# Reordering operand preparation at layer ends, weight checks and attention norms in an attention and feed-forward kernel

## The chip, the cores and the metric

The kernel runs on one core of one Trainium2 chip. The metric is device time in microseconds (us). TensorE (PE) multiplies matrices, VectorE (DVE) and ScalarE (ACT) work element by element, GpSimd (POOL) does small and odd work, SyncE (SP) issues DMAs. Each engine executes its own instructions in the order in which the program gives them; engines wait for one another through semaphores.

## What is computed

A transformer block in float32 on `x` of shape 4 x 1024 x 256 (4 sequences, here called blocks 0 to 3): attention with 16 heads, then a gated feed-forward net with ternary weights, each between two layer norms and added to its input.

```python
x = x + layernorm(attention(layernorm(x), Wqkv, Wout))
h = silu(lin(n, w1, s1)) * lin(n, w2, s2)      # n = layernorm(x); 256 -> 1024, gated
h = gelu(lin(h, h1, sh1))                      # 1024 -> 1024, square layer one
h = gelu(lin(h, h2, sh2))                      # 1024 -> 1024, square layer two
x = x + layernorm(lin(h, w3, s3))              # 1024 -> 256
```

`lin` is a product with ternary weights (-1, 0, 1) times a scale for each output.

## The kernel before

**Attention** runs first over all four blocks, paced by exponentials on ScalarE and by TensorE. Side work is kept in chains of `Step`s, each with a `gap` (how many slots must pass since the chain's last step) that `side.take` gives out, one slot at a time, between pieces of the main loop. The function `ending(b, h, copy)` in the attention part makes the chain that projects half `h` of block `b`, normalises it and adds it to `x`: `gather` (statistics, VectorE), `root` (reciprocal root `rstd`, GpSimd, L108), `apply` (for block 3: `nb` on VectorE, L118, then scaling on ScalarE, L123) and `residual` (VectorE, L652). Block 3's chain is still running when the feed-forward part begins: there `side.take` is called once for each group of block 0's gated stage.

**Feed-forward** (`feed_forward`) goes through the blocks; each has four stages.

1. `gated`: 16 groups of 8 matmuls into one of three large PSUM tiles (`pg`, L936), then Silu on ScalarE (`sg`, L938) and the gated product on VectorE (`g`, L939). Lists named `steps` hold what is issued after each group.
2. `Layer.run`, twice: the square layers, by a Strassen-like scheme of seven products (k = 0 to 6) over quarter blocks, in 14 groups g of 16 matmuls (`ph`, L1015), k = g // 2 and r = g % 2 from group 6 on. Every operand is needed as a high and a low half: `high` rounds a raw tile on ScalarE (L906), `low` subtracts that from it on VectorE (L910). The last four groups end in `add`: group 10 and 11 sum PSUM into `w` (block (1, 1) of the output), group 12 and 13 into `u` (block (0, 1)), on VectorE (L1026), and `gelu` follows on ScalarE as two instructions (L1003). Groups 12 and 13 accumulate on in the same PSUM tiles that the sums of groups 10 and 11 read. What is issued after a group is in the lists `steps` and `extra`; `ending(layer, drop)` in the feed-forward part fills `extra` with the halves of output blocks that are ready (`split` gives `high` and `low` of one).
3. `finish`: products with `w3` (`pz`, L1119), first from blocks (0, 0), (1, 0), then (1, 1), (0, 1); then the layer norm and the sum with `x`.

**Checks** run beside this from block 1 on: a piece of a weight is loaded by SP (L1166), cast to int8 on ScalarE (`cast`, L1173) and compared on VectorE (`run`, L1179), 22 pieces in all; `checked(list, casts, runs)` says after which groups. If a weight is not a whole number, the result is computed again in another way; `judge` sums the verdicts in the last layer.

The queues of SP carry the weights of the square layers (`load_factor`, each issued when a product has released its ring), the checks' loads and the stores, in order. The `prepare` steps, spread over `extra`, norm and transpose the next block's input (`cq0hi`, `ck1lo` and the like, L882).

The order of everything is the order in which these functions are called. The group's end in `Layer.run` is:

```python
products(k, r, k == 5)
if k == 3:
    keep_copy("w", r)
elif k == 4:
    straight(1, r, at[r])
else:
    add(*(("w", 1, 1) if k == 5 else ("u", 0, 1)), r)
after(g)
```

Of the kernel before, what the change touches and what calls it, by code (L numbers as in the profile page):

```python
# [40 lines left out]
TPQ = NQ // P  # L41
# [89 lines left out]
def tile_fast(ctx: ExitStack, tc: tile.TileContext, x, wqk, wv, wo, w1, w1s, w2, w2s, h1, h1s, h2, h2s, w3, w3s, out, bad):  # L131
    nc = tc.nc
    B, S, D = x.shape
# [63 lines left out]
    with ExitStack() as actx, ExitStack() as rctx:  # L197
# [404 lines left out]
        def ending(b, h, copy):  # L602

            st = {}

            def transposes(c):
                def run():
                    if c == 0:
                        st["oT"] = work.tile([P, DC, NQ], F32, tag="oT", name=f"oT_{b}_{h}", bufs=1)
                        st["y"] = (both if h else work).tile([P, TPQ, D], F32, tag="y", name=f"y_{b}_{h}", bufs=1)  # L610
                    pt = misc(f"po_{b}_{h}_{c}")
                    for t in range(TPQ):
                        nc.tensor.transpose(pt[:, t * P : (t + 1) * P], on[h][:, t, c * P : (c + 1) * P], ident)
                    copy(st["oT"][:, c, :], pt)

                return run

            def project(t0):
                def run():
                    py = misc(f"py_{b}_{h}_{t0}").rearrange("p (t d) -> p t d", d=D)  # L620
                    for i in range(2):
                        for c in range(DC):
                            by_slots(py[:, i, :], st["oT"][:, c, (t0 + i) * P : (t0 + i + 1) * P], wo_sb[:, c, :], start=c == 0, stop=c == DC - 1)
                    (copy if b == B - 1 else to_scalar)(st["y"][:, t0 : t0 + 2, :], py)

                return run

            def gather(i):
                def run():
                    st["mv"] = norms.gather([st["y"][:, j, :] for j in range(i, i + 2)], i, st.get("mv"))  # L630

                return run

            def root():
                st["ln"] = norms.root(st["mv"])

            def apply(i0):
                def run():
                    if b == B - 1 and i0 == 0:
                        st["to"] = norms.shift(st["ln"])  # L640
                    for i in range(i0, i0 + 2):
                        if b == B - 1:
                            norms.scale(st["y"][:, i, :], st["y"][:, i, :], st["to"], i)
                        else:
                            norms.apply(st["y"][:, i, :], st["y"][:, i, :], st["ln"], i)

                return run

            def residual(i):
                def run():  # L650
                    xr = xs[b][:, h * TPQ + i : h * TPQ + i + 2, :]
                    nc.vector.tensor_add(xr, xr, st["y"][:, i : i + 2, :])  # L652

                return run

            steps = [Step(transposes(c), 1, work=1) for c in range(DC)] + [Step(project(t), 2, heavy=True) for t in range(0, TPQ, 2)]
            tail = (
                [Step(gather(i), 1, False, work=1.6) for i in range(0, TPQ, 2)] + [Step(root, 0, False, work=0.3)]
                + [Step(apply(i), 1, False, work=1.2) for i in range(0, TPQ, 2)] + [Step(residual(i), 1, False, work=1) for i in range(0, TPQ, 2)]
            )  # L660
            if b < B - 1:

                return steps + [Step(lambda: side.add(tail), 0, False)]
            return steps + ([Step(open_ffn, 0, False)] if h == NH - 1 else []) + tail

        class Side:

# [278 lines left out]
        class Layer:  # L946
# [33 lines left out]
            def low(self, k, i):  # L980
                return lambda: self.moving[k].low(i)

            def run(self, q, scale, extra):

                out, at = self.out, {}
                hi, lo = self.high, self.low
# [74 lines left out]
                for g in range(6, 14):  # L1061
                    k, r = g // 2, g % 2
                    if k == 5:
                        space(r)
                    products(k, r, k == 5)
                    if k == 3:
                        keep_copy("w", r)
                    elif k == 4:
# [4 lines that stand above are left out]
                return {n: out[n] for n in ((0, 0), (1, 0), (1, 1), (0, 1))}  # L1073

        class Tail:
# [11 lines left out]
            def apply(self, i0):  # L1087
                if i0 == 0:
                    self.to = norms.shift(self.ln)
                for t in range(i0, i0 + 2):  # L1090
                    norms.scale(self.z[:, t, :], self.z[:, t, :], self.to, t)
# [110 lines left out]
        def feed_forward():  # L1202

            chain = ends[B - 1, NH - 1]
            checks = Checks()
            tails = {}

            def split(o, i):
                return [lambda: o.high(i), lambda: o.low(i)]

            def ending(layer, drop):
                for at in ((0, 0), (1, 0), (1, 1), (0, 1)):
                    layer.out[at] = []
                ops = {at: Operand(layer.out[at], drop) for at in ((0, 0), (1, 0), (1, 1), (0, 1))}
                extra = {g: [] for g in range(14)}
                for g, at, i in ((7, (0, 0), 0), (10, (0, 0), 1), (11, (1, 0), 0), (12, (1, 0), 1)):
                    extra[g] += split(ops[at], i)
                return ops, extra

            def prepared(extra, steps):  # L1220
                for g, k in reversed(list(zip((3, 4, 4, 5, 6, 8, 9), range(7)))):
                    extra[g].insert(0, steps[k].run)

            def checked(steps, casts, runs):
                for g in casts:
                    steps[g].append(checks.cast)
                for g in runs:
                    steps[g].insert(0, checks.run)

            for b in range(B):  # L1230
                last = b == B - 1
                x = {}
                for at in ((0, 0), (1, 0), (0, 1), (1, 1)):
                    x[at] = []
                corner, low = Operand(x[0, 0]), Operand(x[1, 0])
                one = Layer(x, corner, low)
                steps = {g: [] for g in range(NH * HC)}
                if b == 0:
                    for g in steps:
                        steps[g].append(side.take)  # L1240
                    steps[7].append(lambda: until(lambda: "fb" in ffn))
                for g, runs in tails.items():
                    steps[g] += runs
                for g, runs in (
                    (7 if b == 0 else 6, split(corner, 0)), (8 if b == 0 else 7, split(corner, 1)), (9, split(low, 0)), (11, split(low, 1)),
                    (12, [one.t1(0)]), (14, [one.make2(0)]),
                ):
                    steps[g] += runs
                if b == 1:
                    steps[6] += [checks.load, checks.load]  # L1250
                if b:
                    checked(steps, (1, 6, 11), (3, 8, 13))
                gated(x, steps)
                until(lambda: made_factors[0] == len(corners) and "fb" in ffn)
                q = 2 * 7 * b
                ops, extra = ending(one, False)
                if b == 0:
                    for g in range(3, 12):
                        extra[g].append(side.take)
                if b:  # L1260
                    checked(extra, (3, 4, 10), (5, 6, 12))
                if not last:
                    prepared(extra, prepare(2 * b + 2, to_scalar))
                y = one.run(q, scales["h1"], extra)
                until(lambda: not chain[0])
                two = Layer(y, ops[0, 0], ops[1, 0])
                ops, extra = ending(two, True)
                if b:
                    checked(extra, (3, 4), (5, 6))
                if not last:  # L1270
                    prepared(extra, prepare(2 * b + 3, to_scalar))
                else:
                    for g, step in zip((8, 9), judge()):
                        extra[g].append(step.run)
                extra[12] += split(ops[1, 1], 0)
                extra[13] += split(ops[1, 1], 1) + split(ops[0, 1], 0)
                emit([two.t1(0), two.make2(0)])
                two.run(q + 7, scales["h2"], extra)
                tails = finish(b, ops, {0: split(ops[0, 1], 1)})
            assert checks.seen == len(checks.blocks)  # L1280
            side.flush()
# [325 lines left out]
```

## Time and profile before

| | |
|---|---|
| median of 3 runs | 1262.24 us (1261.6 to 1263.4) |
| profiled execution | 1258.22 us, span 1256.4 us |
| mean granted TensorE clock | 0.991 |
| feed-forward part | from about 611 us to the end |
| square layers' sums | L1026 on VectorE, 1.22 us each |
| Gelu pair | L1003 on ScalarE, 1.34 us |
| high half, low half | L906 1.04 us, L910 1.22 us |

A profile line gives start, duration, engine, line of the program, output and inputs with their shapes, and, in brackets, the idle time of the engine before it and what ended it. Chain lines give start, duration, engine, tile and line. Matmul ends are modelled, so successive matmuls seem to overlap.

### The profile page before, as it was taken

The page shows a single profiled execution, that of the slowest core. Times are in us where ns is not written, and L with a number is a line of the kernel's source. Part 1 is how long each engine was busy: PE and PEld are TensorE (multiplying, and loading weights), DVE is VectorE, ACT ScalarE, POOL GpSimd, SP SyncE. Part 2 cuts the span into 40 slices and gives each one's busy share as a digit, 9 for nine tenths or more (in the row PEclk, how much of TensorE's full clock was granted, in tenths as well). Part 3 has the DMA queues.
Part 4 walks back from the last instruction along what each step waited for, and adds up shares of the span by engine and source line. Part 5 has one row for each costly group of instructions (what it writes and reads, how often), then busy time and mean ns, then how long its engine had stood idle before and what let it go on. Part 6 is the DMA issues. An engine that isn't in the chain of part 4 may idle for free.

```text
span 1256.4 us, 20888 instructions
## 1 busy us (share of the span) xinstructions
PE 1194.4 (95%) x7848; PEld 720.9 (57%) x7848; DVE 822.5 (65%) x1448; ACT 887.6 (71%) x1051; POOL 205.8 (16%) x279
## 2 busy tenths in 40 slices
PE   7999999999999999988999999999999999999994
PEld 3333334333333333323568788787888878888783
DVE  3567567776578656766666656767568675784756
ACT  4888788888888888998556564575756756566651
POOL 6211125452444332000000000000000000000000
PEclk9999999999999999999999999999999999999997
DMA  5776645765665665454204341254513545135401
GB/s 145 178 181 161 159 116 138 174 170 147 158 160 144 167 171 130 94 119 142 101 1 138 130 146 61 97 167 152 180 59 108 172 129 190 51 101 184 137 15 37
DMA packets 78670, 163.63 MB, mean 130 GB/s; under 512 B 14688, under 2 KB 40928, under 8 KB 78560
## 3 DMA queue, kind: packets, MB, share of 16 engines
q1 hardware_dynamic: 68624, 131.27, 37.9%
q0 software_dynamic: 9408, 30.42, 7.7%
q8 instruction: 64, 1.05, 0.4%
q10 hardware_dynamic: 528, 0.52, 0.1%
q14 instruction: 46, 0.38, 0.1%
HBM read 98.71 MB, written 29.88 MB: 102 GB/s over the span
## 4 chain that ended last, share of the span: by engine, by line
PE 65%; DVE 12%; ACT 12%; issue 5%; SPq 2%; DMA 2%; POOL 1%; ACTq 0%; POOLq 0%; DVEq 0%
PE ph L1015 25%; PE acc L536 13%; PE s L528 8%; PE pg L936 8%; ACT e L529 6%; PE p L322 4%; DVE lo L910 3%; ACT hi L906 2%; PE py L322 2%; SPq L476 2%; PE pv L322 2%; ACT w L1003 2%; DVE w L1026 2%; DVE u L1026 1%; DVE top L545 1%
## 5 line engine op out<-in xcount | busy, mean ns | idle before, releaser
L529 ACT ACTIVATE e<-s 128x1024 f32<-128x1024 f32 x512 | 482.4, 1034 | 56.9 <-PE s L528 46.9
L536 PE MATMUL acc<-e,vaug 128*32 128x512 f32 x2048 | 256.7, 604 | 2.7 <-POOL vaug L506 2.7
L528 PE MATMUL s<-sq,sk 64*128 64x512 f32 x1024 | 184.3, 441 | 17.5 <-ACT e L529 14.6
L1015 PE MATMUL ph<-hi,sq 128*128 128x512 f32 x448 | 178.3, 398 | 2.6 <-DVE u L1026 2.3
L1015 PE MATMUL ph<-hi,sk 128*128 128x512 f32 x448 | 176.7, 394 | 0.0
L1015 PE MATMUL ph<-lo,sq 128*128 128x512 f32 x448 | 176.6, 394 | 0.0
L1015 PE MATMUL ph<-lo,sk 128*128 128x512 f32 x448 | 176.4, 394 | 0.0
L108 POOL TENSOR_TENSOR rstd<-ve,minus_half 128x4 f32<-128x4 f32 (+1 forms) x34 | 38.0, 1118 | 767.2 <-DVE ve L106 708.2
L528 PEld LDWEIGHTS s<-sq,sk 64*128 64x128 f32 x1024 | 85.3, 184 | 136.6 <-ACT e L529 113.9
L545 DVE TENSOR_TENSOR top<-top,e 128x512 f32<-128x512 f32 x192 | 135.0, 703 | 11.9 <-ACT e L529 6.5
L536 PEld LDWEIGHTS acc<-e,vaug 128*32 128x32 f32 x2048 | 49.4, 109 | 108.2 <-issue 100.2
L910 DVE TENSOR_TENSOR lo<-c,hi 128x1024 fp32r<-128x1024 f32 x48 | 58.4, 1224 | 79.5 <-ACT hi L906 79.5
L1015 PEld LDWEIGHTS ph<-hi,sq 128*128 128x128 f32 x448 | 84.2, 188 | 24.0 <-DVE u L1026 4.0
L910 DVE TENSOR_TENSOR lo<-g,hi 128x1024 fp32r<-128x1024 f32 x48 | 58.8, 1225 | 58.0 <-ACT hi L906 57.7
L1015 PEld LDWEIGHTS ph<-hi,sk 128*128 128x128 f32 x448 | 84.1, 188 | 20.0
L1015 PEld LDWEIGHTS ph<-lo,sk 128*128 128x128 f32 x448 | 84.1, 188 | 19.9
L1015 PEld LDWEIGHTS ph<-lo,sq 128*128 128x128 f32 x448 | 84.2, 188 | 19.1
L1003 ACT ACTIVATE c<-ph,h_scale 128x512 f32<-128x512 f32 x64 | 40.6, 685 | 47.3 <-PE ph L1015 47.3
L938 ACT ACTIVATE sg<-pg,w_scale 128x512 f32<-128x512 f32 x64 | 43.5, 687 | 36.3 <-PE pg L936 33.6
L939 DVE SCALAR_TENSOR_TENSOR g<-pg,w_scale,sg 128x512 f32<-128x512 f32 x64 | 47.8, 747 | 30.1 <-ACT sg L938 30.0
L322 PE MATMUL p<-xT,wqk_sb 128*32 128x512 f32 x512 | 60.8, 593 | 5.6 <-ACT wqk_sb L210 2.6
L1119 PE MATMUL pz<-w_sb,lo 128*128 128x256 f32 x256 | 62.8, 287 | 3.2 <-DVE lo L910 3.2
(189 smaller groups left out, 1785.0 us busy)
## 6 DMA issues: line engine op xcount, KB each, us to landing
sq<-h_f SPq DMA_DIRECT2D x56, 512.0 KB, 3.8
sk<-h_f SPq DMA_DIRECT2D x56, 512.0 KB, 4.4
w<-in_h_dram POOLq DMA_DIRECT2D x32, 256.0 KB, 5.7
h_f<-wr POOLq DMA_DIRECT2D x16, 512.0 KB, 4.4
x<-in_h_dram SPq DMA_DIRECT2D x16, 512.0 KB, 3.5
top_d<-top SPq DMA_DIRECT2D x30, 256.0 KB, 2.3
folded<-top_d SPq DMA_DIRECT2D x30, 256.0 KB, 3.5
h_f<-wr POOLq DMA_DIRECT2D x16, 384.0 KB, 3.7
```

What stands on the lines that cost most here:

```text
L322: nc.tensor.matmul(o[j : j + SLOT, :], w[:, j : j + SLOT], i, **flags)
L528: nc.tensor.matmul(s[:, a, :], stacks[1, g % 2, u][r, c * P : (c + 1) * P], stacks[0, g % 2, u][r, h * NQ : (h + 1) * NQ], start=True, sto ...
L529: nc.scalar.activation(pair(k)[:, u], s, AF.Exp)
L536: nc.tensor.matmul(acc[SLOT * i : SLOT * (i + 1), :], vaug[g % 2][:, c, i, :], pair(k)[:, i // 2, i % 2, :], start=c == 0, stop=c == NT - 1)
L545: nc.vector.tensor_max(top, top if c > 1 else pair(k - 2)[:, :, :, 0:P], pair(k)[:, :, :, 0:P])
L910: nc.vector.tensor_sub(self.lo[i].t, self.raw[i].t, self.hi[i].t.bitcast(F32))
L936: nc.tensor.matmul(p[:, k, :], homes[n][d][:, m * P : (m + 1) * P], half[:, d, :], start=d == j == 0, stop=d == DC - 1 and j == 1)
L938: nc.scalar.activation(sg, p[:, 0, :], AF.Silu, scale=scales["w1"][:, m : m + 1])
L939: nc.vector.scalar_tensor_tensor(x[i, h][c // 2].t[:, c % 2, :], p[:, 1, :], scales["w2"][:, m : m + 1], sg, ALU.mult, ALU.mult)
L1003: nc.scalar.activation(o.t[:, j, :], (o.t if src is None else src)[:, j, :], AF.Gelu, scale=scale[:, m : m + 1])
L1015: nc.tensor.matmul(p[:, j, :], w, half, start=start and c == n == 0, stop=c == HC // 2 - 1 and n == 1, skip_group_check=True,)
L1119: nc.tensor.matmul(p[:, j, :D], half[:, (t0 + j) * P : (t0 + j + 1) * P], homes["w3"][c], start=c == order[0] and n == 0, stop=c == order[ ...
```

## The change

In `Layer.run`, a new list `early` is issued after a group's matmuls and ahead of its sum, copy or Gelu. The halves that `ending` put into `extra` for groups 10, 11 and 12 go into `early`; in layer two also those of block (1, 1), in groups 12 and 13. In block 1's gated stage the casts after groups 1 and 6 and the runs at 3 and 8 are dropped; the checks follow in the later places, one place later each. The first `apply` of block 3's attention endings gets a gap of 2 slots in place of 1; two conditions (`opened.ready` and an `until` before group 5's extra work in block 0) keep the order of what depends on it.

In the streams of the engines, TensorE's and GpSimd's order is unchanged; ScalarE, VectorE and SP have the moves named here.

```diff
@@ -656,12 +656,14 @@
             steps = [Step(transposes(c), 1, work=1) for c in range(DC)] + [Step(project(t), 2, heavy=True) for t in range(0, TPQ, 2)]
             tail = (
                 [Step(gather(i), 1, False, work=1.6) for i in range(0, TPQ, 2)] + [Step(root, 0, False, work=0.3)]
-                + [Step(apply(i), 1, False, work=1.2) for i in range(0, TPQ, 2)] + [Step(residual(i), 1, False, work=1) for i in range(0, TPQ, 2)]
+                + [Step(apply(i), 2 if b == B - 1 and not i else 1, False, work=1.2) for i in range(0, TPQ, 2)] + [Step(residual(i), 1, False, work=1) for i in range(0, TPQ, 2)]
             )
             if b < B - 1:
 
                 return steps + [Step(lambda: side.add(tail), 0, False)]
-            return steps + ([Step(open_ffn, 0, False)] if h == NH - 1 else []) + tail
+            opened = Step(open_ffn, 0, False)
+            opened.ready = lambda: not ends[b, 0][0]
+            return steps + ([opened] if h == NH - 1 else []) + tail
 
         class Side:
 
@@ -980,7 +982,7 @@
             def low(self, k, i):
                 return lambda: self.moving[k].low(i)
 
-            def run(self, q, scale, extra):
+            def run(self, q, scale, extra, early):
 
                 out, at = self.out, {}
                 hi, lo = self.high, self.low
@@ -1063,6 +1065,7 @@
                     if k == 5:
                         space(r)
                     products(k, r, k == 5)
+                    emit(early.get(g, ()))
                     if k == 3:
                         keep_copy("w", r)
                     elif k == 4:
@@ -1213,9 +1216,9 @@
                     layer.out[at] = []
                 ops = {at: Operand(layer.out[at], drop) for at in ((0, 0), (1, 0), (1, 1), (0, 1))}
                 extra = {g: [] for g in range(14)}
-                for g, at, i in ((7, (0, 0), 0), (10, (0, 0), 1), (11, (1, 0), 0), (12, (1, 0), 1)):
-                    extra[g] += split(ops[at], i)
-                return ops, extra
+                extra[7] += split(ops[0, 0], 0)
+                early = {g: split(ops[at], i) for g, at, i in ((10, (0, 0), 1), (11, (1, 0), 0), (12, (1, 0), 1))}
+                return ops, extra, early
 
             def prepared(extra, steps):
                 for g, k in reversed(list(zip((3, 4, 4, 5, 6, 8, 9), range(7)))):
@@ -1248,12 +1251,14 @@
                     steps[g] += runs
                 if b == 1:
                     steps[6] += [checks.load, checks.load]
-                if b:
+                if b == 1:
+                    checked(steps, (11,), (13,))
+                elif b:
                     checked(steps, (1, 6, 11), (3, 8, 13))
                 gated(x, steps)
                 until(lambda: made_factors[0] == len(corners) and "fb" in ffn)
                 q = 2 * 7 * b
-                ops, extra = ending(one, False)
+                ops, extra, early = ending(one, False)
                 if b == 0:
                     for g in range(3, 12):
                         extra[g].append(side.take)
@@ -1261,10 +1266,12 @@
                     checked(extra, (3, 4, 10), (5, 6, 12))
                 if not last:
                     prepared(extra, prepare(2 * b + 2, to_scalar))
-                y = one.run(q, scales["h1"], extra)
+                if b == 0:
+                    extra[5].insert(0, lambda: until(lambda: not chain[0]))
+                y = one.run(q, scales["h1"], extra, early)
                 until(lambda: not chain[0])
                 two = Layer(y, ops[0, 0], ops[1, 0])
-                ops, extra = ending(two, True)
+                ops, extra, early = ending(two, True)
                 if b:
                     checked(extra, (3, 4), (5, 6))
                 if not last:
@@ -1272,10 +1279,11 @@
                 else:
                     for g, step in zip((8, 9), judge()):
                         extra[g].append(step.run)
-                extra[12] += split(ops[1, 1], 0)
-                extra[13] += split(ops[1, 1], 1) + split(ops[0, 1], 0)
+                early[12] += split(ops[1, 1], 0)
+                early[13] = split(ops[1, 1], 1)
+                extra[13] += split(ops[0, 1], 0)
                 emit([two.t1(0), two.make2(0)])
-                two.run(q + 7, scales["h2"], extra)
+                two.run(q + 7, scales["h2"], extra, early)
                 tails = finish(b, ops, {0: split(ops[0, 1], 1)})
             assert checks.seen == len(checks.blocks)
             side.flush()
```

## The prediction

> **What bounds the kernel now.** I read the engine totals first, then who TensorE waited for from 500 us on, then the chain of waits that ended last, then single timelines.
>
> ```profile
> PE 1194.4 (95%) x7848; PEld 720.9 (57%) x7848; DVE 822.5 (65%) x1448; ACT 887.6 (71%) x1051; POOL 205.8 (16%) x279
> ```
>
> TensorE is the bound and the change takes no matmul away, so only its gaps can be won. All the edits lie in the feed-forward part (about 611 us to the end), where it waits little (total us, times, longest):
>
> ```profile
> PE pg L936 <- DVE g L939: 4.5, 4, 2.2
> PE pz L1119 <- DVE lo L910: 3.2, 8, 0.5
> PE ph L1015 <- DVE u L1026: 2.3, 4, 0.6
> PE py L322 <- DVE ck1lo L882: 1.0, 1, 1.0
> ```
>
> Matmul ends are modelled and overlap, so I price a gap from start to start, less the usual pitch (228 ns for 512 columns, about 114 for 256). From the chain, the gated stage of block 1 against that of block 2 (start, us, what):
>
> ```profile
> 777.58 12.71 PE pg L936 x56
> ...
> 791.48 3.91 DMA x<-in_w_dram
> ...
> 797.88 12.75 PE pg L936 x48
> ...
> 934.48 29.05 PE pg L936 x128
> ```
>
> Block 1 spends 33.06 us (777.58 to 810.64) where block 2 spends 29.05: a transfer for the weight check stands in the chain. The end of layer two, block 1:
>
> ```profile
> 906.68 1.23 DVE w L1026
> 907.93 1.34 ACT w L1003 x2
> 909.27 0.95 ACT hi L906
> 910.24 1.23 DVE lo L910
> 911.47 1.15 DVE w L1026
> ...
> 926.62 1.22 DVE lo L910
> ...
> 928.45 1.14 DVE lo L910
> 929.63 4.85 PE pz L1119 x39
> ```
>
> VectorE and ScalarE hand work to and fro: sum, Gelu, high half, low half, next sum. TensorE waits at the end for the last low half. At the end of layer one:
>
> ```profile
> 866.93 1.14 DVE u L1026
> 868.12 29.99 PE ph L1015 x128
> ```
>
> The next layer's second product needs the PSUM bank that the last sum reads. In block 3's attention tail, ScalarE's timeline (start, us; in brackets its idle time):
>
> ```profile
> 640.87 0.69 ACT L938 ACTIVATE sg<-pg,w_scale 128x512 f32<-128x512 f32 x1 [0.18 <-PE pg L936]
> 645.45 1.09 ACT L123 ACTIVATE y<-y,nb,rstd 128x256 f32<-128x256 f32 x2 [3.88 <-DVE nb L118]
> 646.45 0.67 ACT L938 ACTIVATE sg<-pg,w_scale 128x512 f32<-128x512 f32 x1
> ```
>
> ScalarE stood 3.88 us before the norm's scaling, with a Silu (L938) queued behind it that TensorE needed.
>
> [...] Here the granted clock is 0.50 from 797.88 to 801.30 (pitch 427 ns), after a start-to-start gap of only 2.56 us; a gap of 1.43 us (627.52) had no such price. [...] The second `rstd` took 2.04 us beside a low half, the first 1.01[...].
>
> **Part 1: the dropped checks.** Block 1's cast (L1173) after group 6 and its run (L1179) before the work of group 8 go; the other check slots of the gated stages stay, all checks move up by one, and one more falls into block 3's second layer. The cast waited for its DMA, and Silu, product and TensorE waited behind it. Price: the gap's 2.33, then slow pitches 0.36 + 6 x 0.20 + 0.13, **4.0 us**, as 33.06 - 29.05. The two loads stay after group 6 and landed at 796.66 at the latest; the next cast ran at 804.95, so it waits for nothing. The late check (1.05 ScalarE, 1.22 VectorE, its load one place later on SP) sits where blocks 1 and 2 run one without a TensorE gap: 0. Bounds 3.5 to 4.1.
>
> **Part 2: the norms one step later.** No instruction is added. For half 0, `ck1hi` and `ck1lo` no longer stand behind `nb`, which waited for GpSimd (625.89); they can start after `g` at 625.62 instead of 625.97, so `py` starts **0.35** earlier. For half 1, VectorE runs two products, then `nb`; ScalarE runs the next Silu at 642.7 instead of 646.45. Unshifted: products at 644.27 and 644.93; `nb` 645.6; scaling 645.8 to 646.9; high half to 647.85; low half to 649.1; the third product ends at 649.77. The gap at 645.06 stays, that at 647.95 goes, group 15 starts at 649.8 instead of 651.00, and lasts 1.94. The layer starts at 651.74 instead of 653.40: **1.66**. What is late next is that third product, behind the moved scaling. Sum 2.0, bounds 0.5 to 3.
>
> **Part 3: halves ahead of sums.** In groups 10, 11, 12 (13 in layer two) `high` and `low` come before the sum and its Gelu, on both engines; nothing is added. Steps from the trace, start to start: sum to Gelu 1.26, Gelu pair to high 1.25, high to low 1.06, low to the next on VectorE 1.14.
>
> The cost first: the sum of group 10 now follows a low half. In block 1, layer two, `ck1lo` starts at 905.68, so the low half at 906.28 and the sum at 907.42, 0.74 later than 906.68.
>
> Layer one's end: the last sum no longer has a Gelu, a high and a low half before it, and ends before the second product asks. The gap goes: 0.77, 0.73, 0.69, 0.78 by block, each with 0.11 for the first pitch. But in blocks 1 to 3 a cast stands on ScalarE between Gelu 10 and the high half of group 11 (0.95). So the sum of group 11 in block 1: 853.49 + 1.26 + 1.25 + 0.95 + 1.06 + 1.14 = 859.15, ending 860.37; group 13's matmuls, which accumulate into the bank it reads, are due at 860.01. A **new wait** of 0.40 + 0.11 in three blocks; behind it on TensorE is all the rest. Block 0 has no cast: margin 0.6. Net 0.88 + 0.33 + 0.29 + 0.38 = **1.9**.
>
> Layer two's end (no cast): 907.42 + 4.70 = 912.12 for sum 11, ending 0.7 before group 13 needs it; + 1.26 + 1.25 + 1.06 = 915.69, two low halves, sum 12 at 917.96; + 1.25 Gelu + 1.25 high + 1.06 low + 1.13: sum 13 at 922.65; + 1.25 + 1.25 + 1.06 low half at 926.21, `z` at 927.35, last low half 927.95 against 928.36: 0.41. The earlier small gap (920.92) goes, but TensorE only arrives sooner at the same last wait. Block 3 has no `ck1lo`: shift 0.55, gain 0.6. Sum 3 x 0.41 + 0.6 = **1.8**. Nothing to gain or to lose for DMA queues: factor loads follow TensorE.
>
> The steps of part 3 not seen in the trace (order reversed): bounds from -2 (the new wait twice as long, no gain at layer two) to 7.5 (no new wait, 1.2 from each layer two). I take the worked 3.7.
>
> **Sum:** 4.0 + 2.0 + 1.9 + 1.8 = 9.7 us. The profiled execution took 1258.22 (span 1256.4), the runs' median is 1262.24; taken off that, **1252.5**.
>
> **Rivals.** (a) Halves only trade places: the 0.74 and the new wait eat part 3. Then 6.0, 1256.2. For it: the two engines' work between first sum and last low half is the same. Against: fewer hand-overs. (b) The new wait doesn't come and layer two gains 1.15 each: 9.7 + 1.5 + 2.8 = 14.0, 1248.2. (c) The dropped check's wait comes back at the next cast: 9.7 - 4.0 = 5.7, 1256.5; the landing times speak against. (d) Slower: sum 11 comes late for group 13 in all eight layers, by so much that the clock halves after it. At the price of 797.88, 4.0 each, 32 us less the 6 of parts 1 and 2: 1288. It beats the gains from about 1.2 us more a layer than I worked out; against: sum 11 ends within 0.4 of its time, and the halves' blocks have long been ready. (e) The steps move but the waits stay: no change, 1262.
>
> **How the numbers follow.** Mine 0.64, (a) 0.13, (b) 0.08, (c) 0.05, (d) 0.05, (e) 0.05. 0.2% is 2.5 us, about what a measurement of this kernel can tell from no change. Mine, (a), (b), (c) are faster, less 0.02 for a bad draw: 0.88 faster, 0.06 same, 0.06 slower. My own case is 1250 to 1255; to hold 8 in 10 with (a) and a part of (b), 1248.5 to 1257.5.
>
> **What would show it.** Right: block 1's gated stage takes 29 us with the clock at 1.00; no wait of `ph` on the last `u`; a wait of `ph` on `w` of 0.3 to 0.5 in three first layers; last low half of layer two some 22.5 us after its first sum is due (23.0 now); the scaling behind two Silus. Wrong: waits of `ph` on `w` above 1 us or in layer two, a cast waiting for its transfer, or a half clock before 1230 us.

## The result, and the profile after

The change makes the kernel faster. The median fell from 1261.92 us (6 runs, 1257.83 to 1263.4) to 1252.88 us (6 runs, 1248.23 to 1254.59), a ratio of 0.9926 with a 95% interval of 0.9904 to 0.9949. The profiled execution took 1248.23 us with a span of 1246.4 us and a mean granted clock of 0.993, 10.0 us less than the one before.

The engine totals are the same work in a shorter span:

```profile
PE 1190.4 (96%) x7848; PEld 719.9 (58%) x7848; DVE 821.7 (66%) x1448; ACT 888.0 (71%) x1051; POOL 206.0 (17%) x279
```

TensorE's waits from 500 us on (total us, times, longest) show what changed. Line numbers are 2 to 3 higher than before: `pg` 938, `hi` 908, `lo` 912, Gelu 1005, `ph` 1017, sums 1028, `pz` 1122.

```profile
PE pz L1122 <- DVE lo L912: 2.8, 7, 0.5
PE pg L938 <- DVE g L941: 1.4, 2, 0.8
PE ph L1017 <- DVE w L1028: 0.8, 3, 0.4
PE py L322 <- DVE ck1lo L884: 0.7, 1, 0.7
```

`pg` behind `g` fell from 4.5 to 1.4 us, the four waits of `ph` for the last `u` are gone (2.3), and a wait that did not exist, `ph` for `w`, stands in three places: the predicted new one.

The chain of waits of block 1's gated stage is now one piece of TensorE work, with no transfer in it, where there were pieces of 12.71 and 12.75 us with a DMA between them:

```profile
773.60 29.02 PE pg L938 x128
```

The end of layer one in block 1, from the same chain (start, us, what; the dots stand for pieces called "issue", short ones of 0.02 to 0.04 us here, and in the next view for longer stretches too):

```profile
845.47 1.22 DVE w L1028
...
846.72 1.34 ACT w L1005 x2
848.05 0.94 ACT whole L1176
848.99 0.96 ACT hi L908
...
849.97 1.23 DVE lo L912
851.20 1.14 DVE w L1028
...
852.39 37.38 PE ph L1017 x160
```

After the Gelu of group 10 comes the check's cast (`whole`), then the high half, the low half and only then the sum of group 11, for which TensorE waits until 852.39. From there TensorE runs 37.4 us in one piece, over the border to the next layer and its second group, where it used to stop (0.96 us from start to start at 868.12 before). The end of layer two, block 1:

```profile
899.15 1.15 DVE w L1028
...
906.36 0.94 ACT hi L908
...
908.47 1.22 DVE lo L912
909.69 1.15 DVE u L1028
...
919.01 0.68 DVE z L1127
919.70 1.14 DVE lo L912
...
920.88 4.83 PE pz L1122 x39
```

The last low half is still what TensorE waits for, only sooner. And ScalarE's timeline in block 3's attention tail (start, us; idle time in brackets):

```profile
639.94 0.69 ACT L940 ACTIVATE sg<-pg,w_scale 128x512 f32<-128x512 f32 x1 [0.19 <-PE pg L938]
641.75 0.69 ACT L940 ACTIVATE sg<-pg,w_scale 128x512 f32<-128x512 f32 x1 [1.12 <-DVE st L98]
644.84 1.09 ACT L123 ACTIVATE y<-y,nb,rstd 128x256 f32<-128x256 f32 x2 [2.40 <-DVE nb L118]
645.84 1.03 ACT L908 CAST hi<-g 128x1024 fp32r<-128x1024 f32 x1
646.78 0.68 ACT L940 ACTIVATE sg<-pg,w_scale 128x512 f32<-128x512 f32 x1
```

In the traces before and after, VectorE's 1426 and ScalarE's 1042 tile-writing instructions start in the order in which the program gives them, by the tiles they write, so a Silu waits with the scaling that is given ahead of it. Two Silus now precede the scaling. It waits 2.40 us rather than 3.88; the Silu that TensorE needs soonest is no longer behind it, but the third one is.

**Stage by stage.** I cut each trace at the start of the first matmul of a stage. "Layer one" runs to the start of layer two's second group of 16 matmuls (the prediction's "second product", in truth the second half of the first one), so that it holds the wait for the last sum; "end of layer two" runs from the first `pz` to the next block's first `pg` (block 3: to the end of VectorE's last instruction). The changes against before, us:

| stage | before | after | e1 | e2 | e3 | e8 |
|---|---|---|---|---|---|---|
| gated, block 0 | 42.53 | -2.03 | -0.02 | -2.04 | -0.02 | +0.01 |
| gated, block 1 | 33.06 | -4.04 | -4.04 | +0.05 | -1.37 | -4.05 |
| layer one, blocks 0, 1, 2, 3 | 57.74, 57.65, 57.68, 56.48 | -0.87, -0.22, -0.16, -0.15 | 0 to -0.03 | 0 to -0.06 | -0.76, -0.21, -0.16, -0.15 | 0 to +0.01 |
| rest of layer two, blocks 0 to 3 | 49.40, 49.45, 49.49, 48.74 | -0.12, -0.11, -0.10, -0.09 | within 0.01 | within 0.01 | -0.11, -0.12, -0.10, -0.08 | 0 to -0.02 |
| end of layer two, blocks 0, 1, 2, 3 | 16.87, 16.75, 16.73, 29.47 | -0.38, -0.43, -0.44, -0.61 | within 0.02 | within 0.02 | -0.38, -0.40, -0.42, -0.60 | +0.03 to -0.06 |

The column "after" adds up to -9.75 us. The gated stages of blocks 2 and 3 are unchanged (29.06 and 29.03). The spans differ by 10.04: a further 0.57 us arose before the feed-forward part, in code that is the same, and 0.28 went the other way after VectorE's last instruction (5.43 us to the end before, 5.71 after). The attention part reproduces badly: the first `pg` came at 610.87 us before, at 610.30 after, and anywhere between 612.39 and 617.69 in the ten experiments, whose attention code is the same. So single times scatter by some microseconds, while the stages after it repeat to about 0.06 us, but for a half-clock stretch in block 1's gated stage that some executions lack (e3, below). I take the size of an effect from the stages, and the sign for the whole kernel from the timed ratio; e6 shows where one profile's stages mislead.

### The profile page after: what moved, and what is told of

It reads as the page before. It is cut to its first block, busy times and chain, and to the rows that moved or that the text cites. A ratio compares the mean times of both kernels' runs of the same rounds, so it can differ in the third digit from the quotient of the medians.

```text
span 1246.4 us, 20894 instructions
## 1 busy us (share of the span) xinstructions
PE 1190.4 (96%) x7848; PEld 719.9 (58%) x7848; DVE 821.7 (66%) x1448; ACT 888.0 (71%) x1051; POOL 206.0 (17%) x279
## 4 chain that ended last, share of the span: by engine, by line
PE 67%; ACT 11%; DVE 10%; issue 5%; SPq 3%; DMA 2%; POOL 1%; ACTq 0%; POOLq 0%; DVEq 0%
PE ph L1017 27%; PE acc L536 12%; PE pg L938 8%; PE s L528 8%; ACT e L529 6%; PE p L322 4%; SPq L476 3%; DVE lo L912 2%; PE py L322 2%; ACT hi L908 2%; PE pv L322 2%; DVE top L545 1%; PE pz L1122 1%; DVE w L1028 1%; PE po L575 1%
## 5 line engine op out<-in xcount | busy, mean ns | idle before, releaser
L1017 PEld LDWEIGHTS ph<-hi,sq 128*128 128x128 f32 x448 | 84.1, 188 | 21.6 <-DVE w L1028 2.1
```

The source lines that it names most:

```text
L1017: nc.tensor.matmul(p[:, j, :], w, half, start=start and c == n == 0, stop=c == HC // 2 - 1 and n == 1, skip_group_check=True,)
```

## The experiments

My theory: three independent gains, the transfer's wait (4.0), the norms' order (2.0) and the halves' order (3.7, with a new wait that the cast makes). The rivals to be told apart were those of the prediction, and for single parts those that the expectations name.

**e1: only the checks dropped.** In the kernel before, the first of the two casts finds no weight loaded and does nothing, so one check leaves block 1's gated stage; it follows later, and all 22 are made in both kernels.

```diff
-                if b:
+                if b == 1:
+                    checked(steps, (11,), (13,))
+                elif b:
                     checked(steps, (1, 6, 11), (3, 8, 13))
```

> The kernel before with only the two early checks of block 1 dropped. My account: the gated stage of block 1 goes from 33.06 to about 29.05 us with the clock at 1.00, nothing else moves, about 4.0 us in all (ratio 0.9968). Rival (c), the wait comes back at the next cast: the stage stays above 32 us.

Measured: median 1259.66 us, ratio 0.9977 [0.9964, 0.999]. Block 1's gated stage takes 29.02 us, and no other stage moves by more than 0.03. The wait does not come back at the next cast: rival (c) is out.

**e2: only the norms one step later.**

```diff
-                + [Step(apply(i), 1, False, work=1.2) for i in range(0, TPQ, 2)]
+                + [Step(apply(i), 2 if b == B - 1 and not i else 1, False, work=1.2) for i in range(0, TPQ, 2)]
...
+            opened.ready = lambda: not ends[b, 0][0]
...
+                if b == 0:
+                    extra[5].insert(0, lambda: until(lambda: not chain[0]))
```

> The kernel before with only the norms of block 3 one step later (and the two conditions that keep their order). My account: the gated stage of block 0 goes from 42.53 to about 40.5 us, all other stages as before, 2.0 us in all. Rival, the GpSimd wait is only moved to another waiter: the stage keeps 42 us or more.

Measured: 1258.86 us, ratio 0.998 [0.9968, 0.9991]. Block 0's gated stage takes 40.49 us, 2.04 less, and nothing else moves by more than 0.06.

**e3: only the halves ahead of the sums.**

```diff
+                    emit(early.get(g, ()))
...
-                for g, at, i in ((7, (0, 0), 0), (10, (0, 0), 1), (11, (1, 0), 0), (12, (1, 0), 1)):
-                    extra[g] += split(ops[at], i)
+                extra[7] += split(ops[0, 0], 0)
+                early = {g: split(ops[at], i) for g, at, i in ((10, (0, 0), 1), (11, (1, 0), 0), (12, (1, 0), 1))}
...
-                extra[12] += split(ops[1, 1], 0)
-                extra[13] += split(ops[1, 1], 1) + split(ops[0, 1], 0)
+                early[12] += split(ops[1, 1], 0)
+                early[13] = split(ops[1, 1], 1)
+                extra[13] += split(ops[0, 1], 0)
```

> The kernel before with only the halves ahead of the sums. My account: 3.7 us in all. From the first matmul of layer one to the second product of layer two: 0.9 less in block 0, 0.2 to 0.3 less in blocks 1 to 3, with a wait of TensorE for the sum w of group 11 of 0.4 to 0.5 there and none in block 0 (a transfer in block 1's gated stage keeps its 4 us). Layer two's end: 0.4 less per block, 0.6 in block 3. Rival (a), work only trades places: below 1 us in all.

Measured: 1258.97 us, ratio 0.9976 [0.9961, 0.999]. TensorE's waits (lines here are 2 lower than after) have the new wait and the earlier last low half:

```profile
PE pz L1120 <- DVE lo L910: 2.9, 7, 0.5
...
PE ph L1015 <- DVE w L1026: 0.8, 3, 0.4
```

Layer one and layer two gain 1.69 and 1.80 us (with the rest of layer two, which belongs to layer one's wait, as said below). Rival (a), places only traded, is out, and so is (b), since the new wait is there. What I did not expect stands in block 1's gated stage. The check's transfer is still waited for, yet the stage lost 1.37 us. TensorE's timeline:

```profile
799.77 0.50 PE L936 MATMUL pg<-ck1hi,ck0hi 128*128 128x512 f32 x1 [2.10 <-DVE g L939]
...
800.34 0.40 PE L936 MATMUL pg<-ck1hi,ck0lo 128*128 128x512 f32 x1
```

The matmuls after the wait take 0.40 us, where those of before took 0.63 in the same place:

```profile
798.47 0.63 PE L936 MATMUL pg<-ck1lo,ck0hi 128*128 128x512 f32 x1
```

The gap is 2.49 us from start to start here and was 2.56 before; the granted clock after it stays at 1.00 and was 0.50. So 2.7 of the 4.0 us are the wait itself, and 1.4 are a slow clock that it brings only in some executions (e2 has it, with a stage of 33.11 us).

**e8: all checks kept, one load earlier.** This tells the transfer from the work of the check.

```diff
-                    steps[6] += [checks.load, checks.load]
+                    steps[2].append(checks.load)
+                    steps[6].append(checks.load)
```

> The kernel before with all its checks, the first check's load issued after group 2 of block 1's gated stage instead of after group 6. If the stall was the wait for the transfer: the stage falls from 33.06 to 29.1 us and the clock stays 1.00, 4.0 us in all, with no check dropped. If the cast's and the check's own work (1.05 and 1.22 us) made it: it stays above 31 us.

Measured: 1258.04 us, ratio 0.9966 [0.9952, 0.9979]. With all checks in their places, the chain has the whole gated stage of block 1 in one piece:

```profile
781.45 29.02 PE pg L936 x128
```

So the dropped cast and comparison cost TensorE nothing by themselves; the loss was the transfer that came too late for the cast. Moving one load is worth as much as moving the check to a later place.

**e4: layer one's third cast after group 8.** From here on the edits are against the changed kernel.

```diff
-                    checked(extra, (3, 4, 10), (5, 6, 12))
+                    checked(extra, (3, 4, 8), (5, 6, 12))
```

> The changed kernel with the check's cast in the first square layer moved from group 10 to group 8. If the cast between the Gelu of group 10 and the high half of group 11 makes the new wait of TensorE for w: it is gone in blocks 1 to 3, layer one and its boundary are 0.5 to 0.6 us shorter in each, 1.5 us in all against the changed kernel. Rival, the 0.74 us delay of the sum of group 10 is enough alone: the wait stays, less than 0.5 us in all.

Measured: 1250.57 us, ratio to the kernel before 0.9912 [0.9886, 0.9938]. TensorE's waits have no `ph` for `w` any more:

```profile
PE pz L1122 <- DVE lo L912: 2.8, 7, 0.5
PE pg L938 <- DVE g L941: 1.4, 2, 0.8
PE py L322 <- DVE ck1lo L884: 0.7, 1, 0.7
```

Layer one is 0.50, 0.54 and 0.64 us shorter in blocks 1 to 3 than with the change, and within 0.04 us the same in block 0, which has no cast. Without the cast there is no new wait; whether the cast alone makes it, e5 tells.

**e5: the second half of block (0, 0) prepared after group 8** in place of ahead of group 10's sum.

```diff
-                early = {g: split(ops[at], i) for g, at, i in ((10, (0, 0), 1), (11, (1, 0), 0), (12, (1, 0), 1))}
+                extra[8] += split(ops[0, 0], 1)
+                early = {g: split(ops[at], i) for g, at, i in ((11, (1, 0), 0), (12, (1, 0), 1))}
```

> The changed kernel with the halves of block (0, 0)'s second tile issued after group 8 in place of ahead of the sum of group 10. My account: the sum of group 10 starts when its matmuls end (0.55 to 0.75 us sooner), the wait for w of group 11 in blocks 1 to 3 is gone (0.5 each), and the last low half of layer two comes about 0.7 us sooner in each block: 1.5 + 2.7 = about 4.2 us less than the changed kernel, gaps at the end of layer two close to nothing. Rival, ScalarE and VectorE are full through groups 8 to 10 and the sum stays late: below 1 us.

Measured: 1249.38 us, ratio to before 0.9891 [0.9865, 0.9916]. Against the change, layer one is 0.53, 0.79 and 0.59 shorter in blocks 1 to 3, though the cast stands where it stood: the new wait needs both the cast and the later sum of group 10. The end of layer two is 0.88, 0.73, 0.66 and 0.47 shorter, so the rival is out. But layer two of block 3 lost 1.11. Its waits and VectorE's timeline say why:

```profile
PE pz L1122 <- DVE lo L912: 1.1, 4, 0.3
PE pn L1196 <- DVE total L1192: 1.1, 1, 1.1
```

```profile
1199.60 1.22 DVE L912 TENSOR_TENSOR lo<-c,hi 128x1024 fp32r<-128x1024 f32 x1
1200.74 0.18 DVE L1192 TENSOR_REDUCE total<-misses 128x1 f32<-128x30 f32 x1
```

The verdict's sum (`total`) stood behind the moved low half, and a matmul of `judge` (`pn`), next on TensorE, stood for it. My expectation missed that: it looked at the sums and halves and not at the third thing queued on VectorE there. The net gain, summed over the stages, is 3.3 us.

**e7: e5 and e4 together.**

```diff
+                extra[8] += split(ops[0, 0], 1)
...
-                    checked(extra, (3, 4, 10), (5, 6, 12))
+                    checked(extra, (3, 4, 8), (5, 6, 12))
```

> The changed kernel with both moves, the cast after group 8 and the second tile's halves after group 8. If the two moves remove the same wait in layer one: as with the second move alone, within 0.3 us of stage time, or a little worse where group 8 becomes crowded. If they add up: a further 1.5 us less.

Measured: 1250.41 us, ratio to before 0.9905 [0.9868, 0.9942]. Every stage is within 0.06 us of e5's. The two edits remove the same wait. What e5 gives beyond e4 is layer two's end, and 0.25 us more in block 2's layer one.

**e6: the new wait made longer.** The cast after group 10 of layer one is issued three times in blocks 1 to 3; the two repeats write the same values again.

```diff
+                    for _ in range(2):
+                        extra[10].append(lambda: nc.scalar.copy(checks.st["i", checks.made - 1], checks.st[checks.made - 1]))
```

> The changed kernel with the cast after group 10 of layer one repeated twice more (the same cast of the same data) in blocks 1 to 3. My account: each repeat delays the sum of group 11 by 0.95, so TensorE's wait for it grows from 0.4 to about 2.3 us in each of the three layers, 5.7 us in all if the clock stays; if a start-to-start gap of about 2.5 us is enough to halve the clock, as at 797.88 in the kernel before, 1.7 us more in each, up to 10.8 us in all. Rival, the wait for w is not set by this cast: below 2 us.

Measured: 1264.08 us, ratio to before 1.002 [1.0006, 1.0033]: slower than the kernel before. The waits of `ph` for `w` grew from 0.8 us in all to

```profile
PE ph L1017 <- DVE w L1028: 7.3, 3, 2.5
```

Layer one is 3.74, 2.16 and 2.15 us longer than with the change. The windows of 3.41 us right after the three gaps (busy time of TensorE, its weight loads, VectorE, ScalarE and GpSimd; granted clock; DMA share; GB/s):

```profile
858.45:861.86 3.41, 3.41 (x9) 2.75 (x10) 1.13 (x1) 2.25 (x3) 0.00 (x0) 0.59 0.00 0
1014.36:1017.77 3.41, 3.41 (x15) 2.78 (x16) 1.12 (x1) 2.26 (x3) 0.00 (x0) 1.00 0.00 0
1167.62:1171.03 3.41, 3.41 (x15) 2.80 (x16) 1.13 (x1) 2.25 (x3) 0.00 (x0) 1.00 0.02 5
```

The first gap, 2.78 us from start to start, is followed by a slow clock and nine matmuls; the other two, of 2.82 and 2.91, are longer and are followed by the full clock and fifteen. In this execution two of the three gaps cost only the wait, and by its stages it is still 1.7 us faster than the kernel before. It is not typical: its granted clock of 0.991 is the highest of the 20 timed runs, whose mean is 0.987 (0.990 in the 29 runs of the kernel before beside them). The difference of 0.003, over 1260 us, is 3.8 us of lost clock; a stretch of 3.41 us at half clock loses 1.7, so I estimate about two more such stretches per run than in the kernel before. The timed ratios put the loss against the change at 0.0094, about 12 us (7 to 16 with the two intervals), which is about 4 us for each gap (2.4 to 5.4). Rival (d) thus describes a real mechanism, a cast chain that turns the reordering into a loss, and its price of 4.0 us fits the timed runs.

**e9: e5, and `judge`'s first step one group earlier**, to take away e5's loss.

```diff
-                    for g, step in zip((8, 9), judge()):
+                    for g, step in zip((7, 9), judge()):
```

> The changed kernel with the second tile's halves of block (0, 0) after group 8, and the sum of the verdicts in the last layer issued after group 7 in place of 8. In the run without the latter, block 3's second layer was 1.1 us longer, since TensorE's small matmul of the verdicts waited 1.2 us for that sum behind the moved low half. My account: this wait goes, layer two of block 3 comes back to 48.65 us, all other stages as in that run: about 4.4 us of stage time less than the changed kernel. Rival, another wait at the same place in block 3: it stays above 49.5 us.

Measured: 1248.01 us, ratio to before 0.9889 [0.9867, 0.9911]. The wait of `pn` is gone and layer two of block 3 takes 48.62 us again (49.76 in e5). Against the change the stages add up to -4.6 us.

**e10: e9, and the norms' first `apply` three slots after its predecessor** in place of two.

```diff
-                + [Step(apply(i), 2 if b == B - 1 and not i else 1, False, work=1.2) for i in range(0, TPQ, 2)]
+                + [Step(apply(i), 3 if b == B - 1 and not i else 1, False, work=1.2) for i in range(0, TPQ, 2)]
```

> As the run before it in this set, with block 3's norms one step later still (a gap of 3 slots in place of 2). If the gap of 0.95 us that is left before the last gated group of block 0 comes from the scaling ahead of the high half and the Silu on ScalarE: it goes, block 0's gated stage falls from 40.5 to about 39.5 us. Rival, VectorE's own queue makes it: the stage stays within 0.2 us of 40.5, or grows by the residual sums that come later.

Measured: 1246.16 us (1245.93 to 1250.37), ratio to before 0.9886 [0.9863, 0.9909]. Block 0's gated stage takes 39.77 us, 0.73 less than with the change. TensorE's waits:

```profile
PE pg L938 <- DVE g L941: 1.0, 1, 1.0
PE pz L1122 <- DVE lo L912: 0.9, 4, 0.2
```

Two waits of `pg` became one, of 1.15 us above the usual pitch (0.77 and 0.95 with the change): the gap of 0.95 went, but the one before it grew, so the stage missed its 39.5 us. This is the best version that I found: about 5.1 us of stage time better than the change. The intervals of the two ratios overlap at 0.990 to 0.991, so the timed ratio alone does not separate them; the medians are 6.7 us apart, but come from different sets of runs.

## Why the prediction was right, and where it was not

The predicted sum was 9.7 us; the stages give 9.75, and the median came out at 1252.88 against 1252.5. That the medians agree so closely is luck: the six runs scatter from 1248.23 to 1254.59, and the interval of the ratio allows a gain of 6.4 to 12.1 us. The stages are the better test, step by step:

- **Part 1, 4.0:** measured 4.04, alone (e1) and in the change. That nothing takes its place held. The step that was mis-sized is its range. "Bounds 3.5 to 4.1" took the slow clock after the gap for certain, and e3 shows the same wait without it, where the loss is 33.06 - 1.37 - 29.02 = 2.7 us. So the slow clock came after this wait in one execution and not in another; the last section has where the gaps lay, and no run here moved one on purpose.
- **Part 2, 0.35 + 1.66:** measured 2.03. The gap ahead of `py` went from 1.43 to 1.08 us start to start, which is the 0.35. The gap at 647.95 is gone, the one before it stays (0.77 above the pitch), and the last group waits for the third product as worked out: predicted to start at 649.8, which is 648.9 after the 0.57 us of attention and the 0.35, and it started at 648.85.
- **Part 3, layer one, 1.9:** measured 0.87 + 0.22 + 0.16 + 0.15, and 0.12 + 0.11 + 0.10 + 0.09 in the rest of layer two, which is the longer first pitch after the wait that went; together 1.82. That this lies so near 1.9 is in part chance: block 0 gained 0.99 where 0.88 was worked out (0.87 in e3, without the norms' move), block 3 0.24 where 0.38 was. The new wait came in blocks 1 to 3 and not in block 0. It cost 0.39 and 0.41 above the pitch in blocks 1 and 2, as worked out, and 0.52 in block 3, where I had assumed the same. There group 11 lasts 3.71 us in place of block 1's 3.76, and the sum of group 10 starts 0.99 us after group 11 begins in place of 0.95; these are 0.09 of the 0.13 by which block 3 waits longer than block 1.
- **Part 3, layer two, 3 x 0.41 + 0.6:** measured 0.38, 0.43, 0.44 and 0.61. TensorE's group 11 starts 8.35 us earlier than before; shifted by that, the sum of group 10 at 899.07 is the 907.42 that was predicted, and the last low half at 919.61 is 927.96 against 927.95. From the time at which the first sum was due, 22.5 us pass to the end of the last low half, as predicted.
- **The rivals:** (a), (b) and (c) are excluded by e3, the waits after and e1, and (e), no change at all, by the result. (d) is real but begins well beyond the change's 0.4 to 0.5 us: at 2.6 us a block (e6) it costs 2.2 to 3.7 us in each by the profile, 8.05 in all, and about 12 by the timed ratios, and there the gain turns into a loss. The half clock that stands before 1230 us after the change, at 136.83, lies in the attention part, where before has one at 139.12.

## What to carry to other kernels

When one engine's queue has to serve two waiters, count what stands between a result and its next user, in order, for every instruction in that stretch: the sums here came out to a tenth of a microsecond from the start-to-start steps of the same trace, and the expectation that missed most (e5) had left out one instruction. A wait for a transfer can be cured at the transfer (one load a few groups earlier, e8: 29.01 us) as well as by moving the work behind it (e1: 29.02). A move into free time for one stage (the halves ahead of the sum) can be one place too late for another instruction; moving the intruder (e4) or the first of the moved items (e5) further ahead is then the next step to try.

## What the runs showed of the hardware that I had not expected

Gaps of TensorE of nearly the same length had different consequences. Start-to-start gaps of 2.56 (before), 2.58 (e2) and 2.78 us (e6, block 1) were followed by half clock (0.50 from 797.89 to 801.30 before, 3.41 us), which cost 1.4 to 1.6 us; gaps of 2.49 (e3), 2.82 and 2.91 us (e6) were followed by a clock of 1.00. Length alone does not decide between 2.5 and 2.9 us, and such a price is a chance and not a constant.

The place of the gap tells five of the six cases apart. Within a trace, the half-clock stretches start whole multiples of 3.413 us apart:

| trace | half clock from, us | apart, in 3.413 us |
|---|---|---|
| before | 139.12, 797.89, 1241.63 | 193, 130 |
| after | 136.83, 1232.51 | 321 |
| e2 | 14.8, 21.6, 540.4, 591.6, 803.25 | 2, 152, 15, 62 |

Before and after the clock is 0.50 in them; the last one goes on to the end of the span and each of the others lasts 3.41 us. e2's first four are known to a tenth of a microsecond. Where the multiples lie in the span differs: 139.12 is 2.59 us above a whole number of 3.413, 136.83 is 0.30 above and 803.25 is 1.1 above. I counted on in steps of 3.413 us from 797.89 before, 803.25 in e2 and 859.04 in e6 (there the matmul of 859.01 is the first with a longer pitch, and the clock is 0.51 from 859.00 to 862.40). The ends of the other steps are therefore estimates. With TensorE idle from one usual pitch (0.23 us, from 29.02 us for 128 matmuls) after the last matmul's start, the gaps fall like this:

| gap | idle, us | end of a step near it | longest idle time in one step | then |
|---|---|---|---|---|
| before | 795.56 to 797.88 | 797.89 | 2.3 | half clock |
| e2 | 799.76 to 802.11 | 799.84, 803.25 | 2.3 | half clock |
| e6, block 1 | 855.89 to 858.45 | 859.04 | 2.6 | half clock |
| e6, block 2 | 1011.77 to 1014.36 | 1012.64 | 1.7 | full clock |
| e6, block 3 | 1164.94 to 1167.62 | 1166.24 | 1.4 | full clock |

The three gaps that lay in one step (but for 0.08 us in e2) were followed by half clock from the end of that step on, and the two that the end of a step cut were not. In e2 the pitch grows from 0.23 to 0.43 us at about 803.25, which is 1.1 us after its gap has ended. Five cases agree, but no run moved a gap against the steps on purpose, e3's gap is not among them, and no threshold is claimed.

The half-clock stretches also go with the scatter of the runs. In the 20 timed runs of e2 the time falls as the granted clock rises (correlation -0.93; -0.90 in the 20 of e6). In the attention part such stretches come in differing number: one in the profiles that reach the first `pg` by 610.9 us (before and after, with a granted clock of 0.991 and 0.993 over the span), four in e2, at 14.8, 21.6, 540.4 and 591.6, which reaches it at 617.19 us (0.988). Which wait of the attention part brings them was not tried.
